# A graph layer on one core: its edge network's first product as eight small tiles, another setup order, and 13 more picks

## The chip, the core and the metric

One Trainium2 core runs the program: TensorE (PE) for products, VectorE (DVE), ScalarE (ACT), GpSimd (POOL) and SyncE (SP, which here only issues transfers). The metric is the device time in microseconds of one execution; three runs give a median. The profile is of one more execution, whose own time is given beside it.

## What is computed

6,250 nodes with 64 features `x`, 200,000 edges sorted by target node `dst`. Per edge a small network of the 32 edge attributes gives 9 weights; the source row is multiplied into a 9 x 64 outer product and summed by target; then a product with `W_tp`, a gate from `node_vec`, a residual and a layer norm.

```python
w = silu(edge_attr @ W1 + b1) @ W2 + b2                 # 32 -> 64 -> 9
msg = einsum('ef,em,fmg->eg', x[src], edge_sh * w, W_tp)
agg = segment_sum(msg, dst, N) / sqrt(E / N)            # AVG_DEG of 16
gamma, beta = split(silu(c[:, None] @ Wn1 + bn1) @ Wn2 + bn2, 2)
out = layernorm(x + agg * (1 + gamma) + beta)
```

## The kernel before, in words

Edges stand in 98 groups (`NBLK`) of 16 tiles (`KB`) of 128 edges; the last group has 11 tiles. The main loop (from L603) does one block `i` per group, software-pipelined, with the order on each engine written out by hand (`manual_schedule`): each engine works through its instructions in the order in which the program names them, and waits where data or a buffer isn't there yet. A buffer is named by pool and tag; a new tile of a tag waits for all readers of the old one. In PSUM the tags are `p1` (two banks, one buffer), `pz` (two buffers), `px` (two), `s` and `r` (one each).

Source rows come to the tiles in three ways:

- **Gathers** (`gather`, L89 to 95): one indirect DMA of 128 rows from GpSimd for each tile, six groups ahead (`AHEAD`), into seven buffers `hs`. GpSimd does nothing else in the loop. There are 1192.
- **Picks** (`pick`, L463 to 486): the last 3 or 4 tiles of a group (`picked(g)`, L50) are made by TensorE. `x` is held as a high and a low part (`xs`), 7 x 7 slices. The key of an edge, a row's place, is compared with a counter to a one-hot matrix (`hots`, L456 to 461, VectorE, 1.04 us each); 14 products of 128 x 448 (L475) add up in `px`; VectorE masks (L484) and reduces (L486) into `hs`. There are 355. Keys are worked out at the start for all groups, transposed, stored to memory (`kd`), loaded back to all partitions (`load_keys`) and copied to PSUM (`keys`, ScalarE).
- **Single rows** by SyncE (`load_rows`) for the first tile of every sixth group.

The edge network of a group: `hidden` (L398) multiplies the attributes by `W1`. The 128 rows of `ea` are four quarters of edges with 32 attributes each; `w1bd` holds `W1` four times, block-diagonally, so that each of two products takes 64 rows (two quarters), all 128 columns and 512 edges, into one of `p1`'s two banks (L403). `hidden_act` applies silu on ScalarE to both banks at once (L411). `second` (L415) multiplies by `W2` (L420) into a tile of tag `s`, ScalarE adds the bias; `weights` (L425) transposes (L430), multiplies by `sh` (L436) and by the near one-hot of the target into `a` (L442). `windows` (L494) sums source rows times `a` over each tile into windows of 8 nodes (L504), and ScalarE copies them to `zt` (L514, eight copies). Every second block `project` (L530) multiplies two groups' windows by `W_tp` into `pt`, a tile of tag `p1` (L543); ScalarE copies it, `turn` transposes it back into `pt` (L549), and `halves` (L520) splits it: ScalarE reads `pt` (L524), then VectorE (L525). `nodes` (L582) does the node work: the gate's product, `place` (L559), and every fourth block `bring` (L576) with `finish` (VectorE, L670 to 683, and a square root on ScalarE); the gate's last step is L356.

A block in order on TensorE: first pick of group i+1 with the node work between its products; `hidden(i+2)`; `second(i+1)`; `windows(i)`; `project` in odd blocks; second pick with the transposes of `weights` and `turn` between its products; the other picks. On VectorE: gate and finish, two hots of group i+2, mask and reduce of the first pick, the other hots, `weights`, the `halves`, then the remaining masks.

`setup` (from L134) does once: small loads, the keys, `xs`, the picks of group 0, and what blocks 0 and 1 need. GpSimd's gathers of six groups start there.

Of the kernel before, what the change touches and what calls it, by code (L numbers as in the profile page):

```python
# [7 lines left out]
F32 = mybir.dt.float32  # L8
# [7 lines left out]
P = 128  # L16
# [33 lines left out]
def picked(g):  # L50

    return Q - (3 * g % 8 < 3)
# [7 lines left out]
def gnn_resnorm_kernel(ctx: ExitStack, tc: tile.TileContext, x, src, dst, dst_row, ea, sh, cn,  # L60
# [18 lines left out]
    with ExitStack() as fast:  # L79
# [54 lines left out]
        def setup(temp):  # L134
# [4 lines left out]
            for q in range(4):  # L139
                nc.sync.dma_start(w1bd[q * D:(q + 1) * D, (q % 2) * H:(q % 2 + 1) * H], w1)  # L140
            nc.sync.dma_start(src_i[:, AHEAD * KB:], src[:, AHEAD * KB:])
            xb_r = xb.rearrange("p j f -> p (j f)")
            row_i = xb_r[0:1, 0:NBLK * KB].bitcast(I32)
            nc.scalar.dma_start(row_i, dst[0:1, :])
            first_i = temp.tile([NBLK, KB], I32)
            nc.scalar.dma_start(first_i, dst[0].rearrange("(g k) -> g k", k=KB))
            cn_j = temp.tile([NJ, P], F32)
            nc.scalar.dma_start(cn_j, cn)
            for s in range(2):
                nc.scalar.dma_start(b1c[s * H:(s + 1) * H, :], b1.unsqueeze(1))  # L150
# [3 lines left out]
            for h0, h1 in ((0, 2), (2, 4), (4, 7)):  # L154
                nc.scalar.dma_start(xk[:, h0:h1, :], x_v[:, h0:h1, :])
            load(0)
            for s in range(2):
                nc.sync.dma_start(w2p[s * H:(s + 1) * H, s * M:(s + 1) * M], w2)
            nc.sync.dma_start(dst_i, dst)
# [14 lines left out]
            one = temp.tile([1, 1], F32)  # L174
            nc.vector.memset(one, 0.0)
            one_o = temp.tile([1, 1], F32)
            nc.scalar.activation(one_o, one, AF.Silu)
            row_f = xb_r[0:1, NBLK * KB:2 * NBLK * KB]
            nc.scalar.copy(row_f, row_i)
            first_t = temp.tile([NBLK, KB], F32)  # L180
            nc.scalar.copy(first_t, first_i)
# [5 lines left out]
            nc.vector.tensor_add(ident2, ident[:, 0:F], ident[:, F:P])  # L187
            zero = temp.tile([P, 1], F32)
            nc.vector.memset(zero, 0.0)
            for k in range(2):  # L190
                nc.vector.memset(ht[k][H:H + 1], 1.0)
            nc.vector.memset(wtc2[F:P, 4], 0.0)
            ones1 = temp.tile([1, P], F32)
            nc.vector.memset(ones1, 1.0)
            nc.vector.memset(eps, EPS)
            nc.vector.tensor_copy(nk, nk_i)
            nc.vector.tensor_copy(wi, n_i[:, 0:W])
            nc.vector.tensor_copy(li, n_i[:, 0:J])


            zt_r = zt.rearrange("p a c k w -> p (a c k w)")
            s_f, kp, kh, rest, t0, t1 = [zt_r[:, k * C:(k + 1) * C] for k in range(6)]
            ti = [t.bitcast(I32) for t in (t0, t1)]
            s_f = s_f.rearrange("p (g k) -> p g k", k=Q)
            nc.vector.tensor_copy(s_f[:, 0:NBLK - 1, :],
                                  src_i.rearrange("p (g k) -> p g k", k=KB)[:, 0:NBLK - 1, KB - Q:])
            nc.vector.tensor_copy(s_f[:, NBLK - 1, :], src_i[:, NT - Q:NT])
            s_f = s_f.rearrange("p g k -> p (g k)")
            nc.vector.tensor_scalar(ti[0], s_f, 2675.0, None, op0=ALU.mult)
            nc.vector.tensor_scalar(ti[0], ti[0], 17, None, op0=ALU.logical_shift_right)  # L210
            nc.vector.tensor_copy(kp, ti[0])
            nc.vector.scalar_tensor_tensor(rest, kp, -float(J * J), s_f, op0=ALU.mult, op1=ALU.add)
# [16 lines left out]
            for c in range(KB // 4):  # L229
                for s in range(2):  # L230
                    q = c * D + s * M
                    nc.sync.dma_start(b2c[q:q + M, :], b2.unsqueeze(1))
# [626 lines left out]
```

## Time and profile before

| what | value |
|---|---|
| three runs | 1520.66, 1521.2, 1521.42 us; median 1521.2 |
| profiled execution | 1521.78 us, of it 1519.9 us in the span shown |
| granted TensorE clock, mean | 0.983 |
| busy: TensorE, VectorE, ScalarE, GpSimd | 1438.0, 1135.4, 526.1, 1129.3 us |
| gathers (L91), picks' products (L475) | 1192 at 946 ns, 4970 records |
| end of the first pick in the setup | 31.98 us |
| first window product of group 1, 5, 51, 62, 95, 97 | 70.17, 135.17, 809.55, 967.81, 1472.36, 1502.01 us |

A line of the groups gives line, engine, operation, output <- input, partitions x elements, count, then busy time and mean of one, then the engine's idle time before it and what ended most of it. A line of the timeline gives start, duration, engine, line, operation, output <- input, count, and in brackets the idle time before it with its releaser. Matrix products in fp32 appear as two records each. Ends of products are modelled, so a product's cost is better read from start to start.

### The profile page before, as it was taken

The page shows a single profiled execution, that of the slowest core. Times are in us where ns is not written, and L with a number is a line of the kernel's source. Part 1 is how long each engine was busy: PE and PEld are TensorE (multiplying, and loading weights), DVE is VectorE, ACT ScalarE, POOL GpSimd, SP SyncE. Part 2 cuts the span into 40 slices and gives each one's busy share as a digit, 9 for nine tenths or more (in the row PEclk, how much of TensorE's full clock was granted, in tenths as well). Part 3 has the DMA queues.
Part 4 walks back from the last instruction along what each step waited for, and adds up shares of the span by engine and source line. Part 5 has one row for each costly group of instructions (what it writes and reads, how often), then busy time and mean ns, then how long its engine had stood idle before and what let it go on. Part 6 is the DMA issues. An engine that isn't in the chain of part 4 may idle for free.

```text
span 1519.9 us, 34363 instructions
## 1 busy us (share of the span) xinstructions
PE 1438.0 (95%) x10810; PEld 1192.7 (78%) x10810; DVE 1135.4 (75%) x1987; ACT 526.1 (35%) x1335; POOL 1129.3 (74%) x1201
## 2 busy tenths in 40 slices
PE   4998999999999999999999999989998998999995
PEld 2787888888888788888888888878777887878784
DVE  5686777877877878777777877768677777687773
ACT  4223342433423333332423424424233333333331
POOL 7777777777777777777777777777777777777772
PEclk9999999999999999999999999999999999999997
DMA  6422232222222222222322222222222222222210
GB/s 171 95 56 63 54 76 53 64 59 70 65 56 72 58 63 71 60 63 54 74 59 55 72 52 63 71 54 61 53 72 53 59 55 71 52 55 59 73 29 15
DMA packets 90939, 96.16 MB, mean 63 GB/s; under 512 B 37161, under 2 KB 51451, under 8 KB 90748
## 3 DMA queue, kind: packets, MB, share of 16 engines
q0 software_dynamic: 38144, 39.14, 13.4%
q1 hardware_dynamic: 51842, 53.09, 12.1%
q8 instruction: 88, 1.44, 0.4%
q10 hardware_dynamic: 762, 1.64, 0.3%
q14 instruction: 103, 0.84, 0.2%
HBM read 92.04 MB, written 1.73 MB: 62 GB/s over the span
## 4 chain that ended last, share of the span: by engine, by line
PE 57%; POOL 18%; issue 9%; SPq 5%; DMA 5%; DVE 4%; ACT 2%; DVEq 0%; POOLq 0%; ACTq 0%
PE px L475 41%; POOL hs L91 18%; PE pz L504 5%; DMA hs<-in_x_dram,src_i 4%; PE p L403 3%; SPq L106 3%; PE pt L543 3%; PE p L420 2%; SPq L101 2%; PE p L430 1%; PE ps L559 1%; PE ps L589 0%; ACT st L411 0%; DVE hot_k L460 0%; DVE xm L484 0%
## 5 line engine op out<-in xcount | busy, mean ns | idle before, releaser
L91 POOL DMA_INDIRECT hs<-in_x_dram,src_i x1192 | 1128.0, 946 | 364.3 <-issue 330.7
L475 PE MATMUL px<-xs,hot_k 128*128 128x448 f32 x4970 | 1090.6, 372 | 9.4 <-DVE xs L294 8.8
L475 PEld LDWEIGHTS px<-xs,hot_k 128*128 128x128 f32 x4970 | 896.8, 189 | 93.9 <-issue 10.9
L484 DVE SCALAR_TENSOR_TENSOR xm<-li,jl,px 128x448 f32<-128x448 f32 x355 | 240.3, 677 | 203.6 <-PE px L475 202.0
L460 DVE TENSOR_TENSOR hot_k<-pk,nk 128x896 fp32r<-128x896 f32 x355 | 370.6, 1082 | 3.1 <-ACT pk L454 3.1
L411 ACT ACTIVATE st<-p,b1c 128x1024 f32<-128x1024 f32 x98 | 109.5, 1118 | 405.4 <-PE p L403 405.1
L486 DVE TENSOR_REDUCE hs<-xm 128x64 f32<-128x448 f32 x355 | 220.1, 620 | 12.2
L514 ACT COPY zt<-pz 64x160 f32<-64x160 f32 (+2 forms) x784 | 213.5, 272 | 40.6 <-PE pz L504 28.0
L504 PEld LDWEIGHTS pz<-a,hs 128*64 128x64 f32 x3126 | 110.2, 142 | 68.1 <-issue 61.2
L504 PE MATMUL pz<-a,hs 128*64 128x72 f32 x3126 | 124.6, 234 | 27.0 <-DMA hs<-in_x_dram,src_i 11.5
L442 DVE TENSOR_TENSOR a<-oh,p 128x1152 f32<-128x1152 f32 x98 | 132.7, 1354 | 3.3
L436 DVE TENSOR_TENSOR p<-p,sh 128x72 f32<-128x72 f32 x196 | 47.0, 240 | 100.9 <-ACT rt L546 45.2
L403 PE MATMUL p<-ea,w1bd 64*128 64x512 f32 x392 | 113.3, 655 | 0.0
L565 ACT COPY carry<-ps 128x128 f32<-128x128 f32 x48 | 12.8, 266 | 273.4 <-PE ps L559 273.4
L420 PEld LDWEIGHTS p<-st,w2p 128*32 128x32 f32 x784 | 15.8, 108 | 83.2 <-issue 39.0
L420 PE MATMUL p<-st,w2p 128*32 128x256 f32 x784 | 63.5, 396 | 7.8 <-DVE xb L356 7.8
L680 ACT ACTIVATE var<-var,eps 128x2 f32<-128x2 f32 (+1 forms) x25 | 7.4, 295 | 179.2 <-DVE var L679 179.2
L543 PE MATMUL pt<-zt,wtc 128*64 128x128 f32 x960 | 64.3, 281 | 2.6 <-ACT zt L514 1.7
L543 PEld LDWEIGHTS pt<-zt,wtc 128*64 128x64 f32 x960 | 55.0, 142 | 3.8 <-ACT zt L514 1.9
L454 ACT CAST pk<-kr 128x384 f32<-128x384 f16 (+1 forms) x98 | 53.8, 549 | 2.2 <-DMA kr<-kd 2.2
L430 PE MATMUL p<-ident,p2s 128*128 128x128 f32 x196 | 53.3, 273 | 0.0
L403 PEld LDWEIGHTS p<-ea,w1bd 64*128 64x128 f32 x392 | 30.0, 187 | 28.7 <-issue 28.0
(122 smaller groups left out, 529.0 us busy)
## 6 DMA issues: line engine op xcount, KB each, us to landing
hs<-in_x_dram SPq DMA_DIRECT2D x2048, 0.2 KB
ea<-in_ea_dram SPq DMA_DIRECT2D x49, 512.0 KB
hs<-in_x_dram,src_i POOLq DMA_INDIRECT x1192
kr<-kd SPq DMA_DIRECT2D x49, 256.0 KB
sh<-in_sh_dram SPq DMA_DIRECT2D x49, 144.0 KB
cb<-cn_d SPq DMA_DIRECT2D x12, 128.0 KB
out_dram<-o SPq DMA_DIRECT2D x24, 64.0 KB
gam<-in_x_dram ACTq DMA_DIRECT2D x2, 448.0 KB
```

Of the source, the lines that this page charges most:

```text
L91: hs_dma[g] = [nc.gpsimd.indirect_dma_start(out=hs[g][:, t - g * KB, :], out_offset=None, in_=x, in_offset=bass.IndirectOffsetOnAxis(ap=sr ...
L403: nc.tensor.matmul(p1[:, i, :], w1bd[i * 64:(i + 1) * 64, :], e[i * 64:(i + 1) * 64, :], start=True, stop=True)
L411: nc.scalar.activation(st[g], p1_t.pop(g), AF.Silu, bias=b1c)
L420: nc.tensor.matmul(p2[g][c * D:(c + 1) * D, 0, :].rearrange("p (i e) -> p i e", i=2), w2p, s[:, :, c * P:(c + 1) * P], start=True, stop=True)
L442: nc.vector.tensor_mul(a[g], oh_t.pop(g)[:, :, None, :].to_broadcast([P, KB, M, W]), sw.unsqueeze(3).to_broadcast([P, KB, M, W]))
L460: nc.vector.tensor_tensor(hot_k[g, t], pk_t[g][:, t, None, :].to_broadcast([P, J, P]), nk.unsqueeze(2).to_broadcast([P, J, P]), op=ALU.is_ ...
L475: nc.tensor.matmul(px.rearrange("p f l -> p (f l)"), hot_k[g, t][:, h, :], xs[i][:, h].rearrange("p f l -> p (f l)"), start=(h == 0 and i ...
L484: nc.vector.scalar_tensor_tensor(xm, li[:, None, :].to_broadcast([P, F, J]), jl[:, c:c + 1], px, op0=ALU.is_equal, op1=ALU.mult)
L486: nc.vector.tensor_reduce(hs[g][:, tiles(g) - q + t, :], xm, AX.X, ALU.add)
L504: mm = nc.tensor.matmul(pz[v * F:(v + 1) * F, k // 2].rearrange("p m w -> p (m w)"), hsg[:, k0 + k, :], ag[:, k0 + k].rearrange("p m w -> ...
L514: nc.scalar.copy(z[h * F:(h + 1) * F, 0:5 - h, k0 + v:k0 + n:2, :].rearrange("p m k w -> p k m w"), pz[v * F:(v + 1) * F, 0:(n + 1 - v) // ...
L543: nc.tensor.matmul(pt[h * F:(h + 1) * F, 0, 0:P], wtc2[:, c, :], z[h][:, c], start=(c == 0), stop=(c == 4))
```

## The change

`hidden` becomes eight products of 32 rows and 64 columns of the array with 256 edges each; each quarter of the edges has a bank of its own, two in `p1` and two in buffers of tag `pz`. The silu is three instructions. In the block it stands behind the second pick. `picked` gives 368 picks. The setup asks for `x` first, makes the keys of groups 0 and 1 with a diagonal and a product of ones (`keys_first`) and the others' later through memory (`keys_rest`), and reads rows of `dst` broadcast by DMA. Output stores are issued at the start of the next block. At the end, `windows(96)` stands ahead of the last picks, the last windows are done in reverse order with VectorE taking half of the copies, and the odd last projection uses tag `r`. Line numbers of the new kernel differ by a few (its `hidden` product is L405).

```diff
 def picked(g):
-    return Q - (3 * g % 8 < 3)
+    return Q - (4 * g % 17 < 4 or g == NBLK - 1)
...
             nc.sync.dma_start(src_i[:, 0:AHEAD * KB], src[:, 0:AHEAD * KB])
+            xk = gam.rearrange("p (h l) f -> p h (l f)", h=J)
+            x_v = x.rearrange("(p h l) f -> p h (l f)", h=J, l=J)
+            for h0, h1 in ((0, 1), (1, 2), (2, 4), (4, 7)):
+                nc.scalar.dma_start(xk[:, h0:h1, :], x_v[:, h0:h1, :])
             for q in range(4):
                 nc.sync.dma_start(w1bd[q * D:(q + 1) * D, (q % 2) * H:(q % 2 + 1) * H], w1)
-            nc.sync.dma_start(src_i[:, AHEAD * KB:], src[:, AHEAD * KB:])
-            xb_r = xb.rearrange("p j f -> p (j f)")
...
+            row_i = xb.rearrange("p j f -> p (j f)")[:, 0:NBLK * KB].bitcast(I32)
+            load(0, split=True)
+            nc.sync.dma_start(dst_i[:, 0:2 * KB], dst[:, 0:2 * KB])
+            nc.sync.dma_start(row_i[:, 0:2 * KB], rows(dst[0, 0:2 * KB], P))
...
+            def keys_first(g, kf, tag):
+                pk_t[g] = psum.tile([P, Q, P], F32, tag=tag, name=f"pk{g}")
+                for t in range(picked(g)):
+                    c = (g + 1) * Q - picked(g) + t
+                    d0 = NBLK * KB + c * P
+                    dg = xb.rearrange("p j f -> p (j f)")[:, d0:d0 + P]
+                    nc.vector.tensor_scalar(dg, ident, kf[:, c:c + 1], None, op0=ALU.mult)
+                    nc.tensor.matmul(pk_t[g][:, t, :], ones, dg, start=True, stop=True)
...
+            def split(h):
+                xh = gam[:, h * J:(h + 1) * J, :].rearrange("p l f -> p f l")
+                nc.scalar.copy(xs[0][:, h], xh)
+                nc.vector.tensor_sub(xs[1][:, h], xh, xs[0][:, h].bitcast(F32))
+            kf = keys_of(0, LB)
+            keys_first(0, kf, "r")
+            hots(0, 0, 1)
+            for h in range(J):
+                split(h)
+                if h == J // 2:
+                    hots(0, 1, 2)
+            one = temp.tile([1, 1], F32)
+            nc.vector.memset(one, 0.0)
+            nc.scalar.activation(one, one, AF.Silu)
+            pick(0, 0)
+            hots(0, 2, Q)
+            hidden(0)
+            keys_first(1, kf, "s")
+            hots(1, 0, 1)
+            nc.vector.tensor_copy(wi, n_i[:, 0:W])
+            nc.vector.tensor_sub(rel[:, 0:2 * KB], dst_i[:, 0:2 * KB], row_i[:, 0:2 * KB])
+            near(0)
+            pick(0, 1)
+            hots(1, 1, Q)
+            second(0)
+            pick(0, 2, [[lambda: None, lambda: None], weights(0)])
+            hidden(1)
+            nc.sync.dma_start(dst_i[:, 2 * KB:], dst[:, 2 * KB:])
+            nc.sync.dma_start(row_i[:, 2 * KB:], rows(dst[0, 2 * KB:], P))
+            load(LB)
+            keys_rest(keys_of(LB, NBLK))
+            load_keys(LB)
...
-            for h in range(J):
-                xh = gam[:, h * J:(h + 1) * J, :].rearrange("p l f -> p f l")
-                xp = psum.tile([P, F, J], F32, tag="px" if h in (2, 3) else "pz", name=f"x{h}", bufs=2)
-                nc.scalar.copy(xp, xh)
-                nc.scalar.copy(xs[0][:, h], xh)
-                nc.vector.tensor_sub(xs[1][:, h], xp, xs[0][:, h].bitcast(F32))
-                if h == 1:
-                    hidden_act(0)
-                between(h)
-            pick(0, 0)
-            keys(1)
-            hots(1, 0, Q)
-            base(0)
-            near(0)
-            second(0)
-            pick(0, 1)
-            base(1)
...
@@ -393,22 +392,23 @@
             for i in range(n):
                 kr_t[g + i] = kr[:, i, Q - picked(g + i):, :]
-        p1_t = {}
-        def hidden(g, act=True):
+        def hidden(g):
             e = ea_t.pop(g)
-            p1 = psum.tile([P, 2, KB * P // 4], F32, tag="p1", name=f"p1_{g}")
-            for i in range(2):
-                nc.tensor.matmul(p1[:, i, :], w1bd[i * 64:(i + 1) * 64, :], e[i * 64:(i + 1) * 64, :],
-                                 start=True, stop=True)
-            p1_t[g] = p1
-            if act:
-                hidden_act(g)
-        def hidden_act(g):
-            st[g] = work.tile([P, 2, KB * P // 4], F32, tag="st", name=f"st{g}")
-            nc.scalar.activation(st[g], p1_t.pop(g), AF.Silu, bias=b1c)
+            p1 = psum.tile([P, 2, 4 * P], F32, tag="p1", name=f"p1_{g}")
+            bank = [p1[:, i, 0:2 * P] for i in range(2)]
+            bank += [psum.tile([P, 2 * P], F32, tag="pz", name=f"p1_{g}_{i}", bufs=2) for i in range(2)]
+            for q in range(4):
+                eq = e[q * D:(q + 1) * D, :].rearrange("p (c s e) -> p s c e", s=2, e=P)
+                for s in range(2):
+                    nc.tensor.matmul(bank[q][s * H:(s + 1) * H].rearrange("p (c e) -> p c e", e=P),
+                                     w1bd[q * D:(q + 1) * D, (q % 2) * H:(q % 2 + 1) * H], eq[:, s],
+                                     start=True, stop=True)
+            st[g] = work.tile([P, 4, 2 * P], F32, tag="st", name=f"st{g}")
+            nc.scalar.activation(st[g][:, 2], bank[2], AF.Silu, bias=b1c)
+            nc.scalar.activation(st[g][:, 3], bank[3], AF.Silu, bias=b1c)
+            nc.scalar.activation(st[g][:, 0:2], p1[:, :, 0:2 * P], AF.Silu, bias=b1c)
         p2, p2s = {}, {}
...
             p2[g] = psum.tile([P, 2, 2 * P], F32, tag="s", name=f"p2_{g}")
             for c in range(KB // 4):
                 nc.tensor.matmul(p2[g][c * D:(c + 1) * D, 0, :].rearrange("p (i e) -> p i e", i=2), w2p,
-                                 s[:, :, c * P:(c + 1) * P], start=True, stop=True)
+                                 s[:, c // 2::2, c % 2 * P:(c % 2 + 1) * P], start=True, stop=True)
             p2s[g] = work.tile([P, 2 * P], F32, tag="p2s", name=f"p2s{g}")
             nc.scalar.activation(p2s[g], p2[g][:, 0, :], AF.Identity, bias=b2c)
...
             nk = tiles(g)
             hsg, ag = hs.pop(g), a.pop(g)
             z = zs[g] if g in zs else sums(g)
-            for k0 in range(0, nk, ZT):
+            end = g == NBLK - 1
+            for k0 in reversed(range(0, nk, ZT)) if end else range(0, nk, ZT):
                 n = min(ZT, nk - k0)
-                pz = psum.tile([P, ZT // 2, M, W], F32, tag="pz", name=f"pz{g}_{k0}", bufs=2)
+                pz = [psum.tile([P, ZT // 2, M, W], F32, tag="pz", name=f"pz{g}_{k0}", bufs=2)]
+                pz.append(psum.tile([P, ZT // 2, M, W], F32, tag="px", name=f"pz{g}_{k0}_", bufs=2) if end else pz[0])
                 for k in range(n):
                     v = k % 2
-                    mm = nc.tensor.matmul(pz[v * F:(v + 1) * F, k // 2].rearrange("p m w -> p (m w)"),
+                    mm = nc.tensor.matmul(pz[v][v * F:(v + 1) * F, k // 2].rearrange("p m w -> p (m w)"),
                                           hsg[:, k0 + k, :], ag[:, k0 + k].rearrange("p m w -> p (m w)"),
                                           start=True, stop=True)
                     if k0 + k == 0:
@@ -511,9 +515,9 @@
                                 mybir.DependencyClass.Sync, mybir.DependencyReason.DATA), reason="rows of the group")
                 for v in range(2):
                     for h in range(2):
-                        nc.scalar.copy(
+                        (nc.vector.tensor_copy if end and v else nc.scalar.copy)(
                             z[h * F:(h + 1) * F, 0:5 - h, k0 + v:k0 + n:2, :].rearrange("p m k w -> p k m w"),
-                            pz[v * F:(v + 1) * F, 0:(n + 1 - v) // 2, h:M:2, :])
+                            pz[v][v * F:(v + 1) * F, 0:(n + 1 - v) // 2, h:M:2, :])
         r, hot, carry, yt = {}, {}, {}, {}
...
             gs = pair(q)
-            pt = psum.tile([P, 2, 4 * P], F32, tag="p1", name=f"pt{q}")
             z = [zs.pop(g).rearrange("p c k w -> p c (k w)") for g in gs]
             if len(gs) == 1:
+                pr = psum.tile([P, 1, F], F32, tag="r", name=f"pr{q}")
                 for c in range(5):
-                    nc.tensor.matmul(pt[:, 0, 0:F], z[0][:, c], wtc2[:, c, :], start=(c == 0), stop=(c == 4))
-                halves(q, pt[:, 0, 0:F].unsqueeze(1))
+                    nc.tensor.matmul(pr[:, 0], z[0][:, c], wtc2[:, c, :], start=(c == 0), stop=(c == 4))
+                halves(q, pr)
                 return []
+            pt = psum.tile([P, 2, 4 * P], F32, tag="p1", name=f"pt{q}")
             for c in range(5):
                 for h in range(2):
                     nc.tensor.matmul(pt[h * F:(h + 1) * F, 0, 0:P], wtc2[:, c, :], z[h][:, c],
...
@@ -623,38 +630,40 @@
                     hots(i + 2, 2, Q)
                 if 3 <= i <= 5:
                     reach(i - 3)
-                if i + 2 < NBLK:
-                    hidden(i + 2)
                 if i + 1 < NBLK:
                     second(i + 1)
-                if i < NBLK - 2:
+                if i < NBLK - 1:
                     windows(i)
-                turn = project(i // 2) if i % 2 == 1 else []
+                turn = project(i // 2) if i % 2 == 1 and i < NBLK - 1 else []
                 if i % 4 == 1 and i - 1 < NJ:
                     gate_hidden(i - 1)
                 if i + 1 < NBLK:
                     pick(i + 1, 1, [weights(i + 1), turn])
+                if i + 2 < NBLK:
+                    hidden(i + 2)
+                if i == NBLK - 2:
+                    sums(i + 1)
+                    turn = project(i // 2)
+                    ps = psum.tile([P, 2 * P], F32, tag="s", name="ps_l")
+                    pick(i + 1, 2, [turn])
+                    more = place(i // 2, ps)
+                    if picked(i + 1) < Q:
+                        for f in more:
+                            f()
+                        more = []
+                    pick(i + 1, 3, [more])
+                    continue
                 for t in range(2, Q):
                     pick(i + 1, t)
-                if i == NBLK - 1:
-                    for f in turn:
-                        f()
-                    ps = psum.tile([P, 4, P], F32, tag="s", name="ps_l")
-                    for f in place(i // 2, ps[:, 0:2].rearrange("p a n -> p (a n)")):
-                        f()
-                    py = psum.tile([P, FB, F], F32, tag="r", name="py_l")
-                    for f in bring(NJ - 3, NJ - 1, py):
-                        f()
-                if i >= NBLK - 2:
-                    windows(i)
-                if i == NBLK - 2:
-                    sums(i + 1)
+            for f in bring(NJ - 3, NJ - 1, psum.tile([P, FB, F], F32, tag="s", name="py_l")):
+                f()
+            windows(NBLK - 1)
             project(NBLK // 2)
-            ps = psum.tile([P, 4, P], F32, tag="s", name="ps_n")
-            for f in place(NBLK // 2, ps[:, 0:2].rearrange("p a n -> p (a n)")):
+            ps = psum.tile([P, 2 * P], F32, tag="p1", name="ps_n")
+            for f in place(NBLK // 2, ps) + bring(NJ - 1, NJ, psum.tile([P, 1, F], F32, tag="r", name="py_n")):
                 f()
-            for f in bring(NJ - 1, NJ, psum.tile([P, 1, F], F32, tag="r", name="py_n")):
-                f()
+            while stores:
+                stores.pop(0)()
     bad_n = nc.values_load(flag_i[0:1, 0:1], min_val=0, max_val=4 * P,
```

## The prediction

> **What bounds the kernel now.** I read the page first (busy time by engine, then the costliest groups), then the timeline of GpSimd alone, then the timeline of all engines in the middle of the run, and last the starts of the window products (L504) of each group against the end of that group's gathers.
>
> ```profile
> PE 1438.0 (95%) x10810; PEld 1192.7 (78%) x10810; DVE 1135.4 (75%) x1987; ACT 526.1 (35%) x1335; POOL 1129.3 (74%) x1201
> L91 POOL DMA_INDIRECT hs<-in_x_dram,src_i x1192 | 1128.0, 946 | 364.3 <-issue 330.7
> L475 PE MATMUL px<-xs,hot_k 128*128 128x448 f32 x4970 | 1090.6, 372 | 9.4 <-DVE xs L294 8.8
> L403 PE MATMUL p<-ea,w1bd 64*128 64x512 f32 x392 | 113.3, 655 | 0.0
> ```
>
> TensorE is at 95%. GpSimd's 74% misleads: each gather has 0.30 us of issue before it, so the queue is full from its first gather to its last:
>
> ```profile
> 2.92 1.11 POOL L91 DMA_INDIRECT hs<-in_x_dram,src_i  x1 [0.97 <-DMA src_i<-in_src_dram]
> 4.33 0.95 POOL L91 DMA_INDIRECT hs<-in_x_dram,src_i  x1 [0.30 <-issue]
> ...
> 1493.22 0.94 POOL L91 DMA_INDIRECT hs<-in_x_dram,src_i  x1 [0.30 <-issue]
> ```
>
> (1493.22 - 2.92)/1191 = 1.251 us a gather. Counting gathers by group (tiles less picks, less one in the groups that SyncE serves), the window product of group 1 starts 36 us after its last gather, that of group 51 (809.55) 11 us after, that of group 62 (967.81) 1.6 us after, and from there to group 95 (1472.36) never more than 6.5. So **TensorE sets the pace up to group 62 and GpSimd from there on**. TensorE's own pace: 674.4 us from group 5 (135.17) to 51, 158.3 from 51 to 62 with 40 picks. A pick costs 2.80 us (blocks that differ by one pick take 13.32 and 16.12). So groups 51 to 95 with their 160 picks would take TensorE 44 x (158.3 - 40 x 2.803)/11 + 160 x 2.803 = 632.9 us; they took 662.8. GpSimd costs 29.9 us there.
>
> Now two blocks of the timeline. An ordinary one (block 48): the first layer L403 comes right after a pick and takes 1.06 us to the second layer L420.
>
> ```profile
> 765.03 1.13 PE L403 MATMUL p<-ea,w1bd 64*128 64x512 f32 x4
> 766.09 0.64 PE L420 MATMUL p<-st,w2p 128*32 128x256 f32 x8
> 766.66 1.22 PE L504 MATMUL pz<-a,hs 128*64 128x72 f32 x32
> ```
>
> Every fourth block (47) also ends two blocks of nodes on VectorE:
>
> ```profile
> 749.33 0.29 DVE L670 TENSOR_TENSOR y<-ps,gam 128x128 f32<-128x128 f32 x1 [0.50 <-PE ps L576]
> 750.88 1.13 PE L403 MATMUL p<-ea,w1bd 64*128 64x512 f32 x4
> 752.42 0.21 DVE L356 TENSOR_TENSOR xb<-xb,ps 128x64 f32<-128x64 f32 x1
> 752.77 0.64 PE L420 MATMUL p<-st,w2p 128*32 128x256 f32 x8 [0.77 <-DVE xb L356]
> 755.59 0.67 PE L475 MATMUL px<-xs,hot_k 128*128 128x448 f32 x2
> 757.93 0.27 PE L549 MATMUL pt<-ident,rt 128*128 128x128 f32 x1
> 758.33 1.35 DVE L442 TENSOR_TENSOR a<-oh,p 128x1152 f32<-128x1152 f32 x1
> 759.60 0.28 DVE L525 TENSOR_TENSOR r<-pt,r 128x128 fp32r<-128x128 f32 x1
> ```
>
> Two things are to be seen. The second layer waits for VectorE's gate (xb, same PSUM slot "s") whether or not the first layer stands before it. And r, the last reader of the projection's PSUM tile pt, ends at 759.88, while the pick that began at 755.59 ends at about 758.76 (four products of 0.2 us behind L549).
>
> **What the Trainium skill says.** "TensorEngine Tiling (Array Packing)", Theoretical Speedup and Gotcha 1: 32 rows give up to 4x, 64 columns up to 2x, and row tiles must write to different PSUM banks; Key Properties: changing the tiling mode drains the array. The trace agrees as far as it goes: L403 (2 tiles) streams 4 x 512 columns in 1.06 us, L420 (4 tiles) 8 x 256 in 0.57; at 0.446 us per 1000 columns of one pass (L475: 448 columns in 0.200) and two passes per record over the tiles, that is 0.91 + 0.15 and 0.46 + 0.11. "TensorE: Matmul & The Clock Gate", Part 3: 4 row tiles reached 3.07x, 3x3 tiles 6.32x; eight tiles are in no row here. "ScalarE: Activation LUTs", What ACT_TABLE_LOAD costs: 280 ns + 0.833 ns per element with a bias pointer; L411's 1118 ns for 1024 fits.
>
> **The change part by part.**
> *First layer (h).* Eight products, 16 records of 256 columns on eight tiles: 16 x 256 x 0.892/8 = 0.457 us, plus 0.11 of filling as at L420: **h = 0.57 us** in place of 1.06. Bounds: 0.50 (hardly any filling) and 0.75 (L504 issues a load and a product every 32.5 ns; 16 of them are 0.52, plus a last tile's 0.23). ScalarE: 2 x 0.49 + 0.71 = 1.69 us in place of 1.12; ScalarE is 65% idle and the second layer wants it a pick and more later, so nothing.
>
> *Its new place,* behind the second pick. The new p1 takes pt's slot, and in odd blocks the built order has it wait for VectorE: r, L525. Behind the waiting TensorE stand the remaining picks.
> - Even blocks, and odd ones without a projection: -1.06 + 0.57 = -0.49. The new banks come free with the copies of L514, which end before the second pick does (769.86 less 1.06 against 769.85): close, but no wait.
> - Block 49 and its like: r ends 0.31 after the pick; -0.49 + 0.31 = -0.18.
> - Finishing blocks up to 47: L403 stood under the gate's wait, so nothing is removed; +0.57, and r is 0.7 to 1.1 late. After 50 there is no gate, but by the trace r ends 0.87 behind the pick's present end, and VectorE's chain doesn't move. Where i+2 has three picks, r comes a hot (1.04) sooner: four early and four late blocks have no stall. Stalls: 8.0 us in 11 blocks, 6.1 in 11.
> - Group 5 to 95: 68 x (-0.49) + 23 x 0.31 + 22 x 0.57 + 14.1 + 1.0 (block 5, L403 under another wait) = **+1.4 us**. The saving of 33 is eaten.
>
> *368 picks.* 13 x 2.80 = **+36.4 us** of TensorE, all between group 5 and 95; VectorE gets 13 x (1.04 + 0.68 + 0.62), off the path beyond what is counted. GpSimd loses 13 x 1.251 = 16.3 us: last gather at 1476.96.
>
> *GpSimd's wait* goes: 29.9 us, if TensorE stays behind. Group 95's gathers then end at 1470.45 - 16.3 = 1454.
>
> *Setup.* x is asked for first, on ScalarE's queue at 0.75 us, not 4.03; keys of two groups need no trip through memory; copies into PSUM (7 x 0.91) go. ScalarE: table load 1.28 and 7 x 0.95 from about 3.4, so the first pick ends near 12.5, not 32. Then VectorE is the bound: 3 x 1.3 for picks, 5 hots at 1.04, masks 1.2, weights 1.9, near and rel 0.7, and the keys of the other groups, 10 steps, 4.5: about 30. Now the trip: transposes and copies 3, store and load of kd 4.6 + 3.7 (13.18 and 18.19 in the chain), then keys, and p2s and the window copies behind them on ScalarE's queue. VectorE needs 8 us more before the last pick of group 1 has its slot. The window product of group 1: 70.17 becomes about 58, **-12.2** (bounds -6 and -17: SyncE's queue gets the small loads that ScalarE had, and 1.6 MB of row and dst). Blocks 1 to 4: 4 x (-0.49) + 0.3 = -1.7.
>
> *End.* Group 97 has three picks, window 96 stands ahead of them, the last transposes lie in a pick. Window 95 to end: 47.5 now. New: 17.2 to window 96 (block 95's four picks, stall and h in it), 10.2 to the end of bring, 17.9 from there (finish on VectorE now stands ahead of its copies): 45.3, **-2.2**.
>
> Sum on the profiled span: 1519.9 - 12.2 - 1.7 + 1.4 + 36.4 - 29.9 - 2.2 = 1511.7. The profiled execution took 1521.78, 1.9 more than its span, and the median is 0.6 below it: **1513.0 us**.
>
> **Rivals.** *(A, forecast)* as above, TensorE 12 us behind GpSimd at group 95: 1505 to 1522; chance 0.50, of it 0.40 faster.
> *(B) GpSimd stays the bound:* r's wait is shorter than read, h nearer 0.5, setup gives more. Last gather 1476.96 + 0.94 + 1.6 to land, then about 17: 1497 span, 1498 us. For it: 12 us is all that is missing. Against: the wait on VectorE is in the built order. 0.25.
> *(C) Slower:* eight tiles don't overlap as four do, in each of 90 blocks between the picks. Each 0.1 us of h is 9 us; from h = 0.70 the sum is above 1523. At 0.75 it is 1529; at 1.06, no gain from tiling, 1557. For it: no row shows eight tiles; mode changes drain. Against: four tiles overlap almost fully in L420. 0.20.
> *(D) No difference:* h of 0.63 to 0.69 or a setup that gives only half, 1518 to 1524; 0.05 beside A's own 0.10.
>
> The likeliest is A, at 1513. The range runs from 1496, just below B, to 1528; outside it lie about 2 in 10. About 0.2%, 3 us, can be told from no change: faster 0.65, same 0.15, slower 0.20.
>
> **What would show it.** The first-layer group at about 0.57 us from its first product to the next pick; TensorE waiting for r in every fourth block for about 1 us, 20 us in all; window 1 near 58; GpSimd's last gather near 1477 and window 95 some 12 us behind its gathers. Wrong if windows again follow their gathers by 2 us (B), or if the first layer takes 0.7 and more (C).

## The result, and the profile after

The changed kernel takes **1555.95 us** (median of four, 1552.85 to 1559.32) against 1520.97 in the same call: a ratio of 1.0233, 95% interval 1.0220 to 1.0246. It is slower by 35 us, where 1513 was forecast. The profiled execution took 1559.32 us, 1557.3 of it in the span. Four of the experiments (numbers 5 to 8) fell on a chip on which the kernel before took 2468 us, and in their traces TensorE stands idle dozens of times, mostly for 3 to 11 us; they say nothing of the whole time, and three of them were run again.

From the page after, the groups that answer to those of before (busy time, mean; then idle time and what ended it):

```profile
PE 1461.8 (94%) x12173; PEld 1221.2 (78%) x12173; DVE 1167.6 (75%) x2047; ACT 570.3 (37%) x1517; POOL 1123.1 (72%) x1188
L91 POOL DMA_INDIRECT hs<-in_x_dram,src_i x1179 | 1121.8, 951 | 361.4 <-issue 327.7
L475 PE MATMUL px<-xs,hot_k 128*128 128x448 f32 x5152 | 1168.3, 377 | 2.1 <-ACT xs L234 1.3
L405 PE MATMUL p<-ea,w1bd 32*64 32x256 f32 x1568 | 68.5, 404 | 29.1 <-DVE r L529 26.0
```

TensorE's busy share hardly moved (95 to 94%). What is new is the idle time in front of the first layer: 26.0 us, ended by VectorE's r. GpSimd is no longer the bound: its last gather starts at 1484.19, and the window product of group 95 follows that group's last gather by 50 us, where it was 1.9.

Where the time went is read from the first window product of a group:

| stretch | before | after | predicted |
|---|---|---|---|
| to group 1 | 70.17 | 70.44 | 58 |
| groups 1 to 5 | 65.0 | 66.7 | 63.3 |
| groups 5 to 95 | 1337.2 | 1374.4 | 1345.1 |
| group 95 to the end | 47.5 | 45.75 | 45.3 |

So 12.4 us of the miss lie in the setup, 3.4 in blocks 1 to 4, 29.3 in the steady run of the loop, and none at the end.

Now the loop. An even block (62) in the timeline of TensorE:

```profile
1020.29 2.25 PE L475 MATMUL px<-xs,hot_k 128*128 128x448 f32 x10
1022.48 0.69 PE L405 MATMUL p<-ea,w1bd 32*64 32x256 f32 x16
1023.09 6.28 PE L475 MATMUL px<-xs,hot_k 128*128 128x448 f32 x30
```

From the first layer to the next pick's product it is 0.61 us, in nearly all 98 blocks 0.61 to 0.63. The trace's starts, record by record, give the rest of the price (ns, the usual value; a pick's product follows a pick's product after 200):

| from, to | before | after |
|---|---|---|
| pick's product, first record of the first layer | 290 | 290 |
| first to last record of the first layer | 540 | 313 |
| last record, next stage | 519 (second layer) | 304 (pick) |
| that pick's first product, its second | none | 308 |
| pick's product, second layer | none | 290 |

So TensorE pays 90 ns to go from untiled to tiled work and some 110 ns to come back. (It is not the change from the pick's type to fp32: an untiled fp32 product between two of a pick's, L430, starts after 200 to 205 ns, and the second of the two follows the first after 515 to 520 in all, where twice 200 and its own 110 make 510. So the 198 ns come with the tiling.) Before, first and second layer shared one visit; now each has its own. The first layer's own cost is 540 + 519 = 1.06 us before, and 90 + 313 + 304 + 108 = 0.82 us now. Inside the 313 ns the first eight records start within 47 ns and the ninth 220 ns behind the eighth: the tiles do run side by side.

A finishing block (87), TensorE and VectorE:

```profile
1393.43 0.27 PE L554 MATMUL pt<-ident,rt 128*128 128x128 f32 x1
1393.46 1.05 PE L475 MATMUL px<-xs,hot_k 128*128 128x448 f32 x4
1395.14 1.35 DVE L442 TENSOR_TENSOR a<-oh,p 128x1152 f32<-128x1152 f32 x1
1396.41 0.28 DVE L529 TENSOR_TENSOR r<-pt,r 128x128 fp32r<-128x128 f32 x1
1396.75 0.69 PE L405 MATMUL p<-ea,w1bd 32*64 32x256 f32 x16 [2.24 <-DVE r L529]
```

The pick is done at about 1394.5, and the third pick could run (experiment 2 puts it here). It doesn't: the first layer stands ahead of it in TensorE's order, and its `p1` tile is free only when r (L529) has read `pt`. The bracket is the price, 2.24 us. From block 51 on it is 2.1 to 2.24 in seven finishing blocks, 1.1 to 1.2 in the five where group i+2 has three picks.

The stretches of 6 us behind two such waits, one of 2.24 us (block 87) and one of 1.16 (block 71) (length, busy time and count by engine, TensorE's granted clock, DMA):

```profile
1396.75:1402.75 6.00, 6.00 (x35) 5.15 (x36) 2.37 (x6) 1.80 (x4) 4.59 (x5) 0.72 0.13 28
1160.73:1166.73 6.00, 6.00 (x43) 5.28 (x44) 3.19 (x6) 1.91 (x4) 4.48 (x6) 1.00 0.11 26
```

The third number from the end is the clock. After 2.24 us of waiting it is 0.72 (one stretch of 3.41 us at half speed), and TensorE gets through 35 records where it did 43. The same 0.72 stands behind six of the seven long waits, and 1.00 behind every wait for r of 1.2 us or less.

And the setup, the records of TensorE that waited, with the pick that followed:

```profile
30.58 1.08 PE L420 MATMUL p<-st,w2p 128*32 128x256 f32 x8 [4.58 <-issue]
43.04 0.47 PE L226 MATMUL p_kt<-ident,zt 128*128 128x128 f32 x1 [5.76 <-DVE zt L208]
48.32 0.51 PE L283 MATMUL p_f<-ident,first_t 98*16 98x98 f32 x2 [3.15 <-ACT first_t L281]
50.02 5.59 PE L475 MATMUL px<-xs,hot_k 128*128 128x448 f32 x14
```

The first pick does end early, at 16.7 us (31.98 before; 12.5 was forecast). Then TensorE waits three times, 13.5 us in all: for the slot "s", which the keys of group 1 hold until VectorE has made their hots; for the keys of the other 96 groups on VectorE; and for `first_t`, which on ScalarE stands behind zeros (L272) that wait for a store of keys. The pick at 50.02 takes 5.59 us in place of 2.80. The clock of the stretches 27 to 32 and 50 to 56 us shows why:

```profile
27.00:32.00 5.00, 1.42 (x9) 0.64 (x10) 3.37 (x4) 0.28 (x1) 3.78 (x4) 0.66 0.12 26
50.00:56.00 6.00, 6.00 (x23) 4.68 (x22) 5.53 (x11) 0.59 (x1) 4.78 (x5) 0.51 0.34 34
```

### The profile page after: what moved, and what is told of

Its sections match the earlier page's. It is cut to its first block, busy times and chain, and to the rows that moved or that the text cites. A ratio compares the mean times of both kernels' runs of the same rounds, so it can differ in the third digit from the quotient of the medians.

```text
span 1557.3 us, 37430 instructions
## 1 busy us (share of the span) xinstructions
PE 1461.8 (94%) x12173; PEld 1221.2 (78%) x12173; DVE 1167.6 (75%) x2047; ACT 570.3 (37%) x1517; POOL 1123.1 (72%) x1188
## 3 DMA queue, kind: packets, MB, share of 16 engines
q10 hardware_dynamic: 576, 1.61, 0.3%
## 4 chain that ended last, share of the span: by engine, by line
PE 64%; DVE 15%; POOL 6%; issue 5%; ACT 4%; DMA 3%; SPq 2%; DVEq 0%; POOLq 0%; ACTq 0%
PE px L475 49%; POOL hs L91 6%; PE pz L508 5%; DVE a L442 4%; PE p L405 3%; DVE hot_k L460 3%; ACT zt L518 3%; PE p L420 3%; DMA hs<-in_x_dram,src_i 2%; DVE p L436 1%; DMA ea<-in_ea_dram 1%; DVE xm L484 1%; DVE hs L486 1%; SPq L106 1%; PE pt L548 1%
## 5 line engine op out<-in xcount | busy, mean ns | idle before, releaser
L475 PE MATMUL px<-xs,hot_k 128*128 128x448 f32 x5152 | 1168.3, 377 | 2.1 <-ACT xs L234 1.3
L475 PEld LDWEIGHTS px<-xs,hot_k 128*128 128x128 f32 x5152 | 932.9, 191 | 127.4 <-issue 44.9
L460 DVE TENSOR_TENSOR hot_k<-pk,nk 128x896 fp32r<-128x896 f32 x368 | 383.6, 1081 | 2.9 <-PE pk L220 2.9
L486 DVE TENSOR_REDUCE hs<-xm 128x64 f32<-128x448 f32 x368 | 228.1, 620 | 12.7
L518 ACT COPY zt<-pz 64x160 f32<-64x160 f32 (+1 forms) x780 | 213.3, 273 | 26.4 <-PE pz L508 16.9
L423 ACT ACTIVATE p2s<-p,b2c 128x256 f32<-128x256 f32 x98 | 46.6, 475 | 310.4 <-PE p L420 309.7
L409 ACT ACTIVATE st<-p,b1c 128x256 f32<-128x256 f32 x98 | 46.6, 475 | 169.7 <-PE p L405 167.3
L405 PE MATMUL p<-ea,w1bd 32*64 32x256 f32 x1568 | 68.5, 404 | 29.1 <-DVE r L529 26.0
L420 PE MATMUL p<-st,w2p 128*32 128x256 f32 x784 | 63.9, 398 | 24.4 <-DVE xb L351 19.5
L405 PEld LDWEIGHTS p<-ea,w1bd 32*64 32x64 f32 x1568 | 23.1, 130 | 61.7 <-DVE r L529 46.4
L411 ACT ACTIVATE st<-p,b1c 128x512 f32<-128x512 f32 x98 | 67.7, 691 | 0.0
L420 PEld LDWEIGHTS p<-st,w2p 128*32 128x32 f32 x784 | 15.9, 108 | 54.1 <-issue 30.9
L454 ACT CAST pk<-kr 128x512 f32<-128x512 f16 (+1 forms) x96 | 55.9, 582 | 0.4 <-DMA kr<-kd 0.4
```

Source lines behind the costliest of these rows:

```text
L405: nc.tensor.matmul(bank[q][s * H:(s + 1) * H].rearrange("p (c e) -> p c e", e=P), w1bd[q * D:(q + 1) * D, (q % 2) * H:(q % 2 + 1) * H], eq ...
L411: nc.scalar.activation(st[g][:, 0:2], p1[:, :, 0:2 * P], AF.Silu, bias=b1c)
L420: nc.tensor.matmul(p2[g][c * D:(c + 1) * D, 0, :].rearrange("p (i e) -> p i e", i=2), w2p, s[:, c // 2::2, c % 2 * P:(c % 2 + 1) * P], sta ...
L460: nc.vector.tensor_tensor(hot_k[g, t], pk_t[g][:, t, None, :].to_broadcast([P, J, P]), nk.unsqueeze(2).to_broadcast([P, J, P]), op=ALU.is_ ...
L475: nc.tensor.matmul(px.rearrange("p f l -> p (f l)"), hot_k[g, t][:, h, :], xs[i][:, h].rearrange("p f l -> p (f l)"), start=(h == 0 and i ...
L486: nc.vector.tensor_reduce(hs[g][:, tiles(g) - q + t, :], xm, AX.X, ALU.add)
```

## The experiments

Theory T: in the loop the new place costs more than eight tiles bring, through the wait for r and the clock behind it, and the visit between two picks is dearer than the stream of the tiles; in the setup the new order loses its gain in its own waits. Rival R1: the eight tiles don't overlap. Rival R2: the 13 picks cost more than 2.80 us each.

**1. Picks back** (354; the new end needs three in group 97).

```diff
-    return Q - (4 * g % 17 < 4 or g == NBLK - 1)
+    return Q - (3 * g % 8 < 3 or g == NBLK - 1)
```

> Only the picks go back (354, the old rule with three for the last group). Theory (everything but the picks sums to about nothing: the first layer gains 0.26 us a block and loses it to waits): 14 picks at 2.80 us come off TensorE's path, 39 us, so about 1518 us, with TensorE within 5 us of GpSimd's gathers at the end. Rival (the new first layer is itself slower and the picks lie beside other work): 1540 to 1556.

Measured: 1528.14 us, ratio to before 1.0044 (1.0027 to 1.0061). T's 1518 was missed. The picks give back 27.8 us and not 39: with this pattern group i+2 has four picks in every finishing block, so all eleven late ones wait over 2 us (nine of them with a fall of the clock behind), and the stretch that holds the wait is 0.85 us longer in the mean than in the changed kernel (9.4 us). Group 95 still stands 11 us behind its gathers. This doesn't yet part the picks from the place: experiment 9 has the picks alone, experiments 2 and 4 another place.

**2. The first layer behind the third pick,** where r has long been read.

```diff
-                if i + 2 < NBLK:
-                    hidden(i + 2)
                 if i == NBLK - 2:
...
                 for t in range(2, Q):
                     pick(i + 1, t)
+                    if t == 2 and i + 2 < NBLK:
+                        hidden(i + 2)
```

> The first layer stands behind the third pick instead of the second, 368 picks kept. Theory (TensorE waits for VectorE's last read of the projection's PSUM tile, 26 us in the finishing blocks and 4 in the others, and its clock drops after waits over 2 us, another 10): these go, 1556 becomes about 1518 to 1525. Rival (VectorE's chain sets the finishing blocks wherever TensorE waits for it): the wait turns up at the following picks or the second layer, 1545 to 1556.

Measured: 1512.82 us, ratio 0.9947 (0.9930 to 0.9963): 43 us less than the changed kernel and below T's range, for one line moved past one pick. The wait for r is gone, and the late stretch from a finishing block's windows to the next falls from 7.16 us (without its picks) to 4.49. Even blocks are unchanged at 2.97, so the visit itself costs the same here.

**3. Two products at the new place.**

```diff
-            for q in range(4):
-                eq = e[q * D:(q + 1) * D, :].rearrange("p (c s e) -> p s c e", s=2, e=P)
-                for s in range(2):
...
+            for i in range(2):
+                nc.tensor.matmul(p1[:, i, :], w1bd[i * 64:(i + 1) * 64, :], e[i * 64:(i + 1) * 64, :],
+                                 start=True, stop=True)
```

> The first layer as two products of 64 rows and 128 columns and one silu again, at the new place, all else as changed. Theory (from pick to pick the eight tiles cost 0.80 us, the two products 1.15): 90 blocks x 0.35 = 31 us more, about 1587. Rival (the eight tiles gain nothing): 1556, or less since no bank of the windows is taken.

Measured: 1601.25 us, ratio 1.0534 (1.0516 to 1.0551). With eight tiles the kernel is 45 us faster at this place, so R1, in the form that the tiles bring nothing, falls. It is more than T's 31. An even block is mostly 0.57 to 0.70 us longer than with eight tiles; of that 1.06 - 0.62 = 0.44 are the products (0.35 was expected), and the rest stands in the picks, a third of whose products follow each other after 206 or 207 ns in place of 200 here. Why they do wasn't found, so not all of the 45 us is the tiles' own.

**4. Eight tiles at the old place,** ahead of the second layer; all else as changed.

```diff
                 if 3 <= i <= 5:
                     reach(i - 3)
+                if i + 2 < NBLK:
+                    hidden(i + 2)
                 if i + 1 < NBLK:
                     second(i + 1)
...
-                if i + 2 < NBLK:
-                    hidden(i + 2)
                 if i == NBLK - 2:
```

> The eight tiles at the old place, ahead of the second layer. Theory (the new place costs the waits for VectorE, the tiles save 0.26 us a block): the waits and the low clock go, and the gate's wait covers the first layer in the finishing blocks up to 48; the windows wait up to 0.3 us for silu to leave their banks: about 1515 to 1525. Rival (the windows' banks make TensorE wait for ScalarE more than VectorE made it): 1540 and more.

Measured: 1508.87 us, ratio 0.9912 (0.9896 to 0.9929), below T's range. 47 us less than the changed kernel, which had lost 35: **the place is the whole loss and more.** In ordinary blocks the stretch from windows to windows is 0.34 us shorter than before; of 1.06 - 0.62 = 0.44 the windows give 0.10 back, waiting for silu to free the banks of `pz` (411 ns behind the second layer in place of 309). In front of the windows of the late finishing blocks it is 0.75 us longer. ScalarE in such a block (63) shows why:

```profile
997.25 0.30 ACT L689 ACTIVATE var<-var,eps 128x2 f32<-128x2 f32 x1 [8.31 <-DVE var L688]
997.57 1.28 ACT L409 ACT_TABLE_LOAD   x1
998.86 0.47 ACT L409 ACTIVATE st<-p,b1c 128x256 f32<-128x256 f32 x1
```

Silu comes behind the square root of the nodes and a table load of 1.28 us (the Trainium skill, "ScalarE: Activation LUTs", What ACT_TABLE_LOAD costs, has 1283 ns for the load: the trace agrees; the page's total of 2.66 us for a switch, with a drain, isn't seen here: silu starts 1.61 us after the start of the square root), and the windows wait 1.12 us for its bank.

**5 and 7, 8.** The kernels of experiments 9, 10 and 12, on the chip of 2468 us: 2469.78, 2544.59 and 2456.16 us, ratios 1.0036 (1.0009 to 1.0062), 1.0278 (1.0205 to 1.0351) and 0.9862 (0.9748 to 0.9977). The first two have the signs of their repeats; the third hasn't. Nothing is built on them.

**6. The eight products issued twice** into the same banks, on the same chip.

```diff
+            for _ in range(2):
             for q in range(4):
```

> The changed kernel with its eight products of the first layer issued twice into the same banks. Theory (eight tiles do overlap; the 0.61 us from the first product to the next pick is 0.46 us of streaming and a fixed 0.15, and 0.19 more are paid once on entering the tiled mode): the second set adds 0.46 us to each of 98 blocks, to 1.07 from the first product to the next pick, 1601 us in all. Rival (the eight tiles overlap badly, so that the 0.61 is all streaming): 0.6 us or more a block, 1615 us and more. Second rival (most of the 0.61 is a fixed cost of a visit): 0.3 us a block, 1585 us.

Measured: 2738.33 us, which can't be used. But where TensorE was not held up, one visit can be read by itself (a row without a bracket in the timeline):

```profile
930.20 1.12 PE L406 MATMUL p<-ea,w1bd 32*64 32x256 f32 x32
931.25 1.08 PE L476 MATMUL px<-xs,hot_k 128*128 128x448 f32 x4
```

32 records take 1.05 us to the next pick, in 53 of 98 blocks 1.04 to 1.06; 16 took 0.62. **The second set costs 0.43 us,** T's 0.46: the eight tiles overlap fully, and 0.19 of the 0.62 is filling. R1 and the expectation's second rival fall.

**9. The kernel before with 368 picks,** nothing else.

```diff
-    return Q - (3 * g % 8 < 3)
+    return Q - (4 * g % 17 < 4 or g == NBLK - 1)
```

> The kernel before with 368 picks and nothing else, again, on a chip where the kernel before takes its 1521 us (in the call before this one it took 2468). Theory (a pick is 2.80 us of TensorE on the path, GpSimd's 29.9 us go): the window product of group 95 at 1478.9, the whole 1526 to 1528 us. Rival (picks cost more than their own products, by later r's and a lower clock): 1535 us and more.

Measured: 1526.43 us, ratio 1.0032 (1.0021 to 1.0044), in T's range; group 95 at 1477.79 for 1478.9, the last gather at 1475.42 for 1476.96. R2 falls: a pick costs no more than its 2.80 us, and GpSimd's wait does go.

**10. TensorE kept busy while it waits:** nine products more ahead of the first layer in the eleven late finishing blocks.

```diff
+                if i % 4 == 3 and 51 <= i < 95:
+                    fill(i + 1, 2, 9)
                 if i + 2 < NBLK:
                     hidden(i + 2)
```

(`fill`, not shown, issues the first product of the third pick, which that pick then overwrites.)

> The changed kernel with nine products more ahead of the first layer in blocks 51, 55 and so on to 91, again, on a chip where the kernel before takes 1521 us. Theory (the waits of over 2 us let the clock fall, some 10 us in all): more work and a faster kernel, 1543 to 1549 us, clock near 0.97 after the waits where it was 0.72. Rival: 1556 us or slightly more.

Measured: 1547.78 us, ratio 1.0175 (1.0158 to 1.0192). **More work, and 8 us less,** in T's range. Block 87, TensorE and VectorE, and the 6 us behind its wait (columns as above):

```profile
1386.06 1.96 PE L471 MATMUL px<-xs,hot_k 128*128 128x448 f32 x9
1387.99 0.28 DVE L540 TENSOR_TENSOR r<-pt,r 128x128 fp32r<-128x128 f32 x1
1388.33 0.69 PE L405 MATMUL p<-ea,w1bd 32*64 32x256 f32 x16 [0.31 <-DVE r L540]
```

```profile
1388.33:1394.33 6.00, 6.00 (x42) 5.13 (x43) 3.21 (x6) 1.80 (x4) 4.48 (x6) 1.00 0.11 23
```

r comes no earlier; the added products (L471) only fill the wait, and the clock behind it is 1.00 for 0.72. Block by block against the changed kernel: the six blocks whose clock had fallen are 1.46 to 1.68 us shorter, 9.5 us together; block 63, which had waited 2.10 us without a fall, is the same; the four with waits of 1.2 us, which the nine products overfill, are 0.53 to 0.62 longer. Ahead of group 51, where both kernels are alike, the changed one has three falls more, in blocks 7, 19 and 35, each behind the wait of the second layer for the gate (1.75 to 1.96 us in eleven blocks, since the first layer no longer stands there; 0.7 before). They make 3.2 us. **The clock cost the profiled run 12.7 us.** That run is the slowest of the four, with the lowest mean clock (0.976; the others 0.977 to 0.981).

Why one wait of 2.1 us brings a fall and another doesn't can be read from the traces. In each, all changes of the granted clock lie on one grid of 3.413 us, to within 3 ns. Take the cells of this grid at full clock in ten traces (before, after and experiments 1 to 4 and 9 to 12), from 140 us to 30 us before the end, and count in each how long no product is on record. All 32 cells with 1.90 us or more are followed by half clock, none of the 3884 with less than 1.75, and 2 of the 12 between. A wait that a grid line cuts does less. Three cells around the wait of block 63 and, above them, two at block 87 (first column after the length: TensorE's busy time):

```profile
1393.90:1397.31 3.41, 1.17 (x20) 0.46 (x18) 3.34 (x8) 1.39 (x2) 2.58 (x3) 1.00 0.31 91
1397.32:1400.73 3.41, 3.41 (x17) 3.01 (x10) 1.11 (x2) 1.80 (x4) 2.50 (x4) 0.50 0.09 19
1035.51:1038.92 3.41, 2.90 (x16) 2.27 (x14) 3.31 (x7) 1.79 (x4) 2.50 (x4) 1.00 0.58 194
1038.92:1042.33 3.41, 1.81 (x22) 1.36 (x23) 3.29 (x6) 1.34 (x4) 2.61 (x3) 1.00 0.16 34
1042.34:1045.74 3.40, 3.40 (x20) 3.19 (x19) 1.45 (x3) 1.11 (x3) 2.68 (x3) 1.00 0.15 34
```

Block 87 idles 2.24 us within one cell, and the next is at 0.50; block 63's 2.10 us are cut into 0.50 and 1.60, and nothing falls. The kernel before has a wait of 2.98 us, cut into 1.80 and 1.17, without a fall. No run moved a wait against the grid on purpose.

**11. Three edits in the setup,** on top of experiment 4.

```diff
-                pk_t[g] = psum.tile([P, Q, P], F32, tag=tag, name=f"pk{g}")
+                if g == 0:
+                    pk_t[g] = psum.tile([P, Q, P], F32, tag=tag, name=f"pk{g}")
+                else:
+                    pk_t[g] = psum.tile([P, 2, 4 * P], F32, tag="p1", name=f"pk{g}")[:, 0, :].rearrange("p (t e) -> p t e", t=Q)
...
             hidden(1)
+            pick(1, 0)
...
-            nc.scalar.copy(zt[F:P, :, 4].rearrange("p a k w -> p a (k w)"),
-                           zero[F:P, :, None].to_broadcast([F, 4, P]))
...
             nc.sync.dma_start(cn_d, cn_s)
+            nc.scalar.copy(zt[F:P, :, 4].rearrange("p a k w -> p a (k w)"),
+                           zero[F:P, :, None].to_broadcast([F, 4, P]))
...
-                pick(i + 1, 0, [nodes(i), more])
+                if i == 0:
+                    for f in nodes(i) + more:
+                        f()
+                else:
+                    pick(i + 1, 0, [nodes(i), more])
```

> The first layer at its old place (1508.9 us), with three edits in the setup: the keys of group 1 in another PSUM slot, so that the second layer of group 0 needn't wait for VectorE's hots; the first pick of group 1 issued ahead of the transposes of the other groups' keys, where TensorE stood idle; first_t copied ahead of the zeros that wait for a store. Theory (the new setup lost its 12 us in these three waits, 4.6, 5.8 and 3.1 us, and in the low clock that came of them): the window product of group 1 at 60 to 64 us in place of 70.4. The whole gains less, as GpSimd is close behind: 1504 to 1507 us. Rival (VectorE and the trip of the keys through memory set the end of the setup, whatever TensorE does): group 1 at 68 to 70, the whole 1508 us.

Measured: **1506.32 us**, ratio 0.9905 (0.9889 to 0.9922), the lowest median of all, though the interval overlaps that of experiment 4. The second layer of group 0 comes at 23.07 (29.84 in experiment 4), and the window product of group 1 at 60.35, ten earlier and in T's range, where the prediction had 58. One wait of the three is left:

```profile
37.01 0.47 PE L229 MATMUL p_kt<-ident,zt 128*128 128x128 f32 x1 [5.68 <-DVE zt L208]
```

At group 51 the lead over experiment 4 is 12.1 us, at group 95 only 2.3: from there GpSimd sets the end again.

**12. The new setup and end alone** (two products, as in experiment 3, at the old place; 354 picks).

```diff
-    return Q - (4 * g % 17 < 4 or g == NBLK - 1)
+    return Q - (3 * g % 8 < 3 or g == NBLK - 1)
...
+                if i + 2 < NBLK:
+                    hidden(i + 2)
                 if i + 1 < NBLK:
                     second(i + 1)
```

> The new setup and the new end alone (two products at their old place, 354 picks), again, on a chip where the kernel before takes 1521 us. Theory (the new setup gains nothing): group 1 at 70 to 71 us, group 51 at 810 to 815, the whole 1519 to 1523 us, set by GpSimd. Rival (it gains its 12 us, and the time was lost in other parts): group 1 near 58, group 51 near 797, the whole still near 1520.

Measured: 1524.01 us, ratio 1.0020 (1.0013 to 1.0027), one us above T's range; group 1 at 68.65 and group 51 at 807.3, a little below T's and far from the rival's 58 and 797. The setup gains 1.5 to 2.3 us of TensorE and costs GpSimd more: its first gather starts at 3.94 us (2.92 before), its eleventh at 18.05 (15.94), and gather 300 at 383.3 in place of 378.7. (In the changed kernel two gathers of the setup take 2.4 and 3.2 us; why wasn't found.)

## Why the prediction was wrong, point by point

The mechanisms were mostly named; two terms of the sum were mis-sized, and the clock was not in it. The time is where rival C had it, but not by C's mechanism: the tiles overlap. By the prediction's own test, from the first product to the next pick, the first layer took 0.62 us, below C's "0.7 and more"; only with both changes of mode is it 0.82. That C's 1557 us for tiles that bring nothing lies beside the measured 1556 is chance.

- **h, the first layer: failed.** "h = 0.57 us" was worked out as stream plus the filling of L420. It measured 0.62, and the stream was right (0.43 for 0.457). What was left out is the visit: 90 ns in and 108 out, since a tiled stage now stands alone between untiled ones, and L403 had stood beside the tiled second layer. The step that failed is "-1.06 + 0.57 = -0.49": it measured **-0.245** (even blocks, experiment 9 against the changed kernel: 3.46 to 3.22 early, 3.22 to 2.97 late), which is 0.82 - 1.06. Over 90 blocks that is 22 us, the largest term. The sentence of the Trainium skill that the prediction named, that changing the tiling mode drains the array ("TensorEngine Tiling (Array Packing)", Key Properties), was the warning; the prediction put no price on it. That the 200 ns are such a drain fits, and wasn't shown separately.
- **The waits: right in place and nearly in size.** Of the late waits for r of 19.6 us, 11 x 1.06 is the time in which the old first layer stood there; 8.0 remain, predicted 6.1. To group 50 the recorded waits are 4.9, predicted 8.0; in the 23 blocks like 49 they are 3.9, predicted 7.1. That the gate's wait to block 47 gives nothing back when the first layer leaves it was foreseen, and came so (1.75 us for 0.7).
- **The clock behind the waits: not in the sum.** The prediction counted a wait at its own length; the falls cost 12.7 us in the profiled run, by experiment 10. The loop of the kernel before had four falls in its trace already, behind waits of 2.3 to 4.8 us ahead of window products. The Trainium skill ("TensorE: Matmul & The Clock Gate", HAM oscillation) says to keep idle gaps of TensorE below about 3.4 us; here 2.1 to 2.24 us were enough in six of seven cases, 1.75 to 1.96 in three of eleven, and 1.2 never. What parts the cases is the idle time within one cell of the clock's grid.
- **What these leave of the loop.** From group 5 to 95 the changed kernel takes 32.3 us more than experiment 9 with the same picks; predicted +1.4. 1.4 + 22.0 (h) + 12.7 (clock) - 1.2 - 3.2 (waits below what was predicted) = 31.7.
- **The setup: failed.** "-12.2 (bounds -6 and -17)" measured +0.3, outside the bounds. "Then VectorE is the bound" overlooked that TensorE's order is fixed: it stood behind "s", behind the keys of 96 groups and behind `first_t`, 13.5 us, and then ran at half clock. Experiment 11 takes two of these away and gets 60.35. Blocks 1 to 4 lost 3.4 more; 4 x 0.245 is h, the rest wasn't tried by itself.
- **368 picks, GpSimd's wait, ScalarE, the end: right.** 36.4 - 29.9 by experiment 9 within 1.1 us at group 95; ScalarE's 1.69 us measured 0.475 x 2 + 0.69 = 1.64 and cost nothing at the new place; the end 45.75 for 45.3. GpSimd's last gather was 7.2 us later than forecast (against experiment 9 its gathers are 6 us late by the 60th already, so most of it is the setup's); it didn't matter, since TensorE was 50 us behind.
- **The range** ended at 1528, about where h = 0.75 alone puts the sum (1529), and had no room for a setup of no gain beside it. Three errors of one sign, h (22 us), the clock (12.7) and the start up to group 5 (15.8), less 4.4 of waits, make 46 us on the profiled span, where 45.6 were measured; the median is 43 over the forecast and 28 beyond the range's edge.

## What to carry to other kernels

An instruction moved on an in-order engine takes its waits with it, and everything behind it pays: ask which buffer it takes and who reads that last, then look one or two stages further on for a place where the reader is long done (43 us here for one pick). Keep tiled stages side by side: the gain of packing is its stream less one visit, and next to another tiled stage 0.2 us of the visit go (0.62 for 0.82). Parts that bring nothing alone can pay together: the picks (1526.4 us) and the new setup and end (1524.0) each lose a little, and with eight tiles at the old place they make 1508.9 of 1521. And an idle engine can pay twice, if its clock falls: look at the granted clock behind each wait, and not at the length of the wait alone.

## What the runs showed of the hardware

- In ten traces TensorE's granted clock changed only on a grid of 3.413 us. Away from setup and end, a cell of it at full clock with 1.90 us or more of idle TensorE was followed by half clock in 32 of 32 cases, one with less than 1.75 in none of 3884. Filling the waits with products whose result isn't used made the kernel 8 us faster.
- Eight tiles of 32 x 64 stream 16 records of 256 fp32 columns in 0.43 us, with 0.19 of filling, and going into and out of tiled work costs 0.09 and 0.11 us.
